# Three one-pass products on split operands in place of the four-pass float32 v projection, with x loaded by pairs

## Chip, cores and metric

One core of one Trainium2 chip. The metric is the time of one execution on the device, in microseconds (us), as the median of several runs; less is better. TensorE is called PE in the profile, VectorE DVE, ScalarE ACT, GpSimd POOL. In this kernel matmuls write tiles in PSUM, and all other tiles lie in SBUF; these are the two on-chip memories. The granted clock is the share of TensorE's full clock that the profile records as allowed.

## The reference

128 batches of a 128 x 512 matrix x go through two layers. All is float32.

```python
# layer 0: r = relu(b + the largest of the 512 columns of adj @ x), one value per row; x = layernorm(x + r)
# layer 1: multi-head attention of 8 heads under the mask adj, then a layer norm added to itself
qkv = x @ w_qkv                                  # 512 -> 3 x 512
attn = softmax(where(adj == 0, -inf, q @ k.T / 8))
o = (attn @ v).reshape(...) @ w_proj + b_proj
o = o + layernorm(o) * ln_gamma + ln_beta
x = layernorm(x + o)
```

The change is about v, the last third of `qkv`.

## The kernel before

The kernel is a software pipeline: in stage s it finishes batch s (transposed scores, attention, projection, two layer norms), computes the scores and the softmax of batch s+1, and the q, k, v of a group of batches 5 stages ahead. TensorE's order is written out by hand; the other engines' orders are made by a scheduler, and each engine runs its own list strictly in order.

```python
for s in range(-A_CONV, B):                 # TensorE's order
    ...
    if here:  eT = transpose_e(s)
    if nxt:   scores(s + 1)                 # psc, mask add, maximum, 8 exponentials
    if dense: qk(u // G, u % G)
    if here:  oT = attend(s, eT)            # pav, copied to oT by ScalarE
    if dense: qk(u // G, KC + u % G)
    if here:  project(s, oT)                # po, then VectorE's o and the layer norms
    if dense: vproj(u // G, u % G)
    if 0 <= t < B: transpose_x(t)
    if w < B: conv(w)

def vproj(g, i):                            # the part that the change rewrites
    xT = xTs[g]
    ...
    for kc in range(KC):                    # KC = 4 float32 matmuls of 512 columns
        nc.tensor.matmul(pv, xT[:, kc, i, :], wqkv_sb[:, kc, 2 * D :],
                         start=(kc == 0), stop=(kc == KC - 1))
    nc.scalar.copy(vs[g][:, i, :], pv)

def scores(b):
    ...
    nc.vector.tensor_tensor(e, psc..., mask_b, op=ALU.add)           # "mask add"
    nc.vector.tensor_reduce(nmax, e, AX.X, ALU.max, negate=True)     # "maximum"
    for j in range(H):                                               # 8 exponentials
        nc.scalar.activation(e[:, j, :], e[:, j, :], AF.Exp, bias=nmax[:, j : j + 1], ...)
    ...

def attend(b, eT):
    ...
    nc.scalar.copy(oT, pav)                 # the copy that project() needs
    return oT

def project(b, oT):
    ...                                     # po = oT @ wproj
    nc.vector.tensor_tensor(o, po, bproj_sb, op=ALU.add)
    nc.gpsimd.tensor_tensor(res, xs[g][:, i, :], o, op=ALU.add)
    stats(...); rstd = rstd_of(...)         # rstd: a small power on GpSimd
    nc.vector.scalar_tensor_tensor(o, o, mv..., gamma_sb, ...)       # "gamma pass"
    nc.vector.scalar_tensor_tensor(o, o, rstd, beta_sb, ...)         # "beta pass"
    nc.vector.tensor_tensor(y, res, o, op=ALU.add)                   # "y"
    stats(...); rstd2 = ...; nc.vector.tensor_scalar(y, ...)         # second layer norm
    nc.sync.dma_start(out[b], y)
```

## Time and profile before

| | before |
|---|---|
| time | 2415.31 us median of 4 runs (2410.86 to 2418.89) |
| TensorE busy | 98% of the span |
| one stage in the steady state | 18.42 us |
| mean granted TensorE clock | 0.995 |

The page's groups have the columns: line, engine, operation, output and inputs, shape and count; then busy us and mean ns of one; then the idle time of the engine just before such instructions, and what ended most of it. Two groups of the kernel before:

```profile
L208 ACT ACTIVATE e<-e,nmax 128x128 f32<-128x128 f32 x1024 | 395.9, 388 | 329.7 <-DVE nmax L205 327.2
L244 PE MATMUL po<-wproj_sb,oT 128*128 128x512 f32 x1024 | 463.1, 595 | 3.7 <-ACT oT L237 3.7
```

### The profile page before, as it was taken

The numbers are of one execution on the slowest core, as the hardware profiler recorded it, in microseconds if no ns is written. First come the engines' busy times: TensorE is split into PE (matmuls) and PEld (weight loads), VectorE is DVE, ScalarE is ACT, GpSimd is POOL, SyncE is SP. The second block draws the span as 40 slices with busy tenths as digits, with TensorE's granted clock in tenths as the row PEclk, the third lists the DMA queues.
The fourth block names the chain that finished last, engine by engine and source line by source line (L and its number), as shares of the span: only waits on it lengthen the run. The fifth ranks groups of instructions, "written<-read, shape, count | busy, mean of one in ns | idle before, by whom it ended". The sixth has DMA issues, their size and how long they took to land.

```text
span 2410.0 us, 27354 instructions
## 1 busy us (share of the span) xinstructions
PE 2368.1 (98%) x9985; PEld 1214.1 (50%) x9985; DVE 1550.2 (64%) x2755; ACT 806.2 (33%) x2689; POOL 333.5 (14%) x422
## 2 busy tenths in 40 slices
PE   7999999999999999999999999999999999999995
PEld 3455555555555555555555555555555555555543
DVE  3576666667666766666676667666666766666556
ACT  1333333333333333333333333333333333333332
POOL 0011111111111111111111111111111111111112
PEclk9999999999999999999999999999999999999998
DMA  5000001000000000000000000000000000000000
GB/s 206 5 31 35 14 31 36 31 31 24 25 31 31 31 36 14 31 35 31 31 21 28 31 31 31 36 14 31 35 31 31 21 29 14 14 14 18 14 18 22
DMA packets 38294, 73.91 MB, mean 31 GB/s; under 512 B 2832, under 2 KB 2960, under 8 KB 38160
## 3 DMA queue, kind: packets, MB, share of 16 engines
q1 hardware_dynamic: 35328, 67.12, 7.8%
q10 hardware_dynamic: 2832, 5.05, 0.6%
q8 instruction: 79, 1.29, 0.2%
q14 instruction: 55, 0.45, 0.1%
HBM read 38.60 MB, written 33.55 MB: 30 GB/s over the span
## 4 chain that ended last, share of the span: by engine, by line
PE 97%; DVE 1%; DMA 0%; ACT 0%; POOL 0%; issue 0%; POOLq 0%; SPq 0%; ACTq 0%; DVEq 0%
PE pq L168 38%; PE pv L183 18%; PE po L244 18%; PE psc L198 6%; PE pav L232 5%; PE ppt L221 5%; PE pa L132 4%; PE ptx L157 2%; DMA xt<-in_x_dram 0%; DVE st L121 0%; ACT e L208 0%; DVE e L214 0%; DVE o L248 0%; POOL res L250 0%; POOL rstd L116 0%
## 5 line engine op out<-in xcount | busy, mean ns | idle before, releaser
L168 PE MATMUL pq<-xT,wqkv_sb 128*128 128x512 f32 x2048 | 945.6, 605 | 0.0
L168 PEld LDWEIGHTS pq<-xT,wqkv_sb 128*128 128x128 f32 x2048 | 368.6, 189 | 408.0 <-issue 392.1
L208 ACT ACTIVATE e<-e,nmax 128x128 f32<-128x128 f32 x1024 | 395.9, 388 | 329.7 <-DVE nmax L205 327.2
L244 PE MATMUL po<-wproj_sb,oT 128*128 128x512 f32 x1024 | 463.1, 595 | 3.7 <-ACT oT L237 3.7
L183 PE MATMUL pv<-wqkv_sb,xT 128*128 128x512 f32 x1024 | 460.3, 592 | 0.0
L187 ACT COPY v<-pv 128x512 f32<-128x512 f32 x128 | 75.0, 586 | 941.7 <-PE pv L183 941.7
L250 POOL TENSOR_TENSOR res<-xt,o 128x512 f32<-128x512 f32 x128 | 162.0, 1266 | 1377.5 <-DVE o L248 984.6
L244 PEld LDWEIGHTS po<-wproj_sb,oT 128*128 128x128 f32 x1024 | 194.6, 191 | 249.6 <-issue 233.5
L183 PEld LDWEIGHTS pv<-wqkv_sb,xT 128*128 128x128 f32 x1024 | 194.6, 190 | 244.9 <-issue 244.9
L116 POOL TENSOR_TENSOR rstd<-ve,mhalf 128x1 f32<-128x1 f32 (+1 forms) x288 | 175.8, 610 | 694.9 <-DVE ve L114 694.5
L248 DVE TENSOR_TENSOR o<-po,bproj_sb 128x512 f32<-128x512 f32 x128 | 88.3, 690 | 269.2 <-PE po L244 269.2
L213 DVE RECIPROCAL rsum<-sums 128x8 f32<-128x8 f32 x128 | 25.7, 200 | 316.1 <-ACT e L208 316.1
L208 ACT ACTIVATION_READ_ACCUMULATOR e<-e,nmax 128x1 f32 x1024 | 191.2, 187 | 0.0
L223 ACT COPY eT<-ppt 128x1024 f32<-128x1024 f32 x128 | 129.6, 1012 | 149.0 <-PE ppt L221 149.0
L214 DVE TENSOR_TENSOR e<-e,rsum 128x1024 f32<-128x1024 f32 x128 | 158.0, 1234 | 4.3
L221 PEld LDWEIGHTS ppt<-ident,e 128*128 128x128 f32 x1024 | 119.4, 141 | 79.7 <-issue 65.0
L232 PEld LDWEIGHTS pav<-eT,v 128*64 128x64 f32 x2048 | 111.0, 138 | 95.5 <-issue 93.7
L205 DVE TENSOR_REDUCE nmax<-e 128x8 f32<-128x1024 f32 x128 | 156.2, 1220 | 3.3
L203 DVE TENSOR_TENSOR e<-psc,mask 128x1024 f32<-128x1024 f32 x128 | 155.0, 1211 | 1.7 <-PE psc L198 1.7
L198 PE MATMUL psc<-qkT 64*128 64x128 f32 x2048 | 150.6, 287 | 0.0
L221 PE MATMUL ppt<-ident,e 128*128 128x128 f32 x1024 | 133.0, 273 | 13.8 <-DVE mv L122 13.8
L175 DVE COPY qkT<-pq 128x512 f32<-128x512 f32 x128 | 88.2, 689 | 85.6 <-PE pq L168 85.3
(34 smaller groups left out, 1745.0 us busy)
## 6 DMA issues: line engine op xcount, KB each, us to landing
xt<-in_x_dram SPq DMA_DIRECT2D x32, 1024.0 KB, 5.4
out_dram<-y SPq DMA_DIRECT2D x128, 256.0 KB, 2.0
wqkv_sb<-in_L_gnn_w_qkv_dram ACTq DMA_DIRECT2D x3, 1024.0 KB, 16.3
wproj_sb<-in_L_gnn_w_proj_dram ACTq DMA_DIRECT2D x1, 1024.0 KB, 23.1
bproj_sb<-in_L_gnn_b_proj_dram ACTq DMA_DIRECT2D x1, 256.0 KB, 17.7
gamma_sb<-in_L_gnn_ln_gamma_dram ACTq DMA_DIRECT2D x1, 256.0 KB, 17.7
beta_sb<-in_L_gnn_ln_beta_dram ACTq DMA_DIRECT2D x1, 256.0 KB, 15.1
adj_sb<-in_adj_dram ACTq DMA_DIRECT2D x1, 64.0 KB, 2.4
```

Source lines behind the costliest of these rows:

```text
L116: nc.gpsimd.tensor_tensor(r, ve, mhalf[:, :n], op=ALU.pow)
L168: nc.tensor.matmul(pq, wqkv_sb[:, kc, c * P : (c + 1) * P], xT[:, kc], start=(kc == 0), stop=(kc == KC - 1),)
L183: nc.tensor.matmul(pv, xT[:, kc, i, :], wqkv_sb[:, kc, 2 * D :], start=(kc == 0), stop=(kc == KC - 1),)
L198: nc.tensor.matmul(psc[:, s, hp, :], qkT[hs, hp, i, :], qkT[hs, KC + hp, i, :], start=True, stop=True,)
L203: nc.vector.tensor_tensor(e, psc.rearrange("p s a m -> p (s a) m"), mask_b, op=ALU.add)
L205: nc.vector.tensor_reduce(nmax, e, AX.X, ALU.max, negate=True)
L208: nc.scalar.activation(e[:, j, :], e[:, j, :], AF.Exp, bias=nmax[:, j : j + 1], accum_out=sums[:, j : j + 1],)
L214: nc.vector.tensor_tensor(e, e, rsum[:, :, None].to_broadcast([P, H, P]), op=ALU.mult)
L221: nc.tensor.transpose(ppt[:, j, :], e[:, j, :], ident)
L232: nc.tensor.matmul(pav[s * HD : (s + 1) * HD, hp, :], vs[g][:, i, h * HD : (h + 1) * HD], eT[:, s * HP + hp, :], start=True, stop=True,)
L244: nc.tensor.matmul(po, oT[:, c, :], wproj_sb[:, c, :], start=(c == 0), stop=(c == KC - 1),)
L250: nc.gpsimd.tensor_tensor(res, xs[g][:, i, :], o, op=ALU.add)
```

## The change

The intent: a float32 matmul makes four passes. Split both operands exactly, x = h + l/4096 and w = wh + wl, each half of at most 12 bits, so that one pass of the faster float32 type (float32r) is meant to be exact. Three products, h·wh and l·wl added in one PSUM bank and d·wd in another, give v by Karatsuba's identity, three passes instead of four: (1 + 1/4096)(h·wh + l·wl) - (h - l)(wh - 4096 wl)/4096 = (h + l/4096)(wh + wl), with d = h - l and wd = wh - 4096 wl. Beside it, x is loaded and normalised by pairs of batches instead of by fours.

```diff
-        xt = xpool.tile([P, G, D], FP, tag="xt", name=f"xt_{g}")
-        nc.sync.dma_start(xt, x[g * G : (g + 1) * G].rearrange("b t d -> t b d"))
+        xt = xpool.tile([P, 2, D], FP, tag="xt", name=f"xt_{p}")
+        nc.sync.dma_start(xt, x[2 * p : 2 * p + 2].rearrange("b t d -> t b d"))
 ...
+    for c in range(KC):                               # weights, once
+        wv = work.tile([P, D], FP, tag="x4", name=f"wv_{c}")
+        nc.scalar.dma_start(wv, w_qkv[c * P : (c + 1) * P, 2 * D :])
+        wh = work.tile([P, D], FP, tag="xh", name=f"wh_{c}")
+        nc.vector.tensor_scalar(wh.bitcast(I32), wv.bitcast(I32), HIGH, None, op0=ALU.bitwise_and)
+        nc.scalar.copy(wv_h[:, c], wh)
+        nc.vector.tensor_tensor(wv_l[:, c], wv, wh, op=ALU.subtract)
+        nc.vector.scalar_tensor_tensor(wv_d[:, c], wv_l[:, c].bitcast(FP), -HALF, wh, ...)
 ...
+    def split_x(b):                                   # every batch
+        nc.scalar.activation(x4, xTs[g][:, :, i, :], AF.Copy, scale=HALF)
+        nc.vector.tensor_scalar(xh.bitcast(I32), x4.bitcast(I32), HIGH, None, op0=ALU.bitwise_and)
+        nc.scalar.activation(h, xh, AF.Copy, scale=1.0 / HALF)
+        nc.gpsimd.tensor_tensor(l, x4, xh, op=ALU.subtract)
+        nc.gpsimd.tensor_tensor(d, h.bitcast(FP), l.bitcast(FP), op=ALU.subtract)
 ...
     def vproj(g, i):
+            nc.tensor.matmul(pv, h[:, kc], wv_h[:, kc], start=(kc == 0), stop=False)
+            nc.tensor.matmul(pv, l[:, kc], wv_l[:, kc], start=False, stop=(kc == KC - 1))
 ...
-                pv, xT[:, kc, i, :], wqkv_sb[:, kc, 2 * D :],
+                pd, d[:, kc], wv_d[:, kc], start=(kc == 0), stop=(kc == KC - 1),
 ...
-        nc.scalar.copy(vs[g][:, i, :], pv)
+        nc.scalar.activation(va, pv, AF.Copy, scale=1.0 + 1.0 / HALF)
+        nc.vector.scalar_tensor_tensor(vs[g][:, i, :], pd, -1.0 / HALF, va, ...)   # "v"
 ...                                  # conv(): statistics after every 2nd batch, not every 4th
-        if i < G - 1:
+        if i == 0:
             return
 ...                                  # work tiles: 1 buffer instead of 2, o and oT 2, y 2 instead of 4
+            if 0 <= s + A_SPLIT < B:
+                split_x(s + A_SPLIT)
```

More of the change, by code (lines that the diff above doesn't have):

```diff
@@ L12 @@
 AX = mybir.AxisListType
+FR = mybir.dt.float32r
+I32 = mybir.dt.int32
 H = 8
@@ L16 @@
 MASKED = -1e30
+HIGH = -4096
+HALF = 4096.0
 @with_exitstack
@@ L58, in tile_adj_resnorm_d2 @@
     const = ctx.enter_context(tc.tile_pool(name="const", bufs=1))
-    xpool = ctx.enter_context(tc.tile_pool(name="xpool", bufs=7))
+    xpool = ctx.enter_context(tc.tile_pool(name="xpool", bufs=9))
     group = ctx.enter_context(tc.tile_pool(name="group", bufs=2))
-    work = ctx.enter_context(tc.tile_pool(name="work", bufs=2))
+    split = ctx.enter_context(tc.tile_pool(name="split", bufs=3))
+    work = ctx.enter_context(tc.tile_pool(name="work", bufs=1))
     small = ctx.enter_context(tc.tile_pool(name="small", bufs=4))
@@ L64, in tile_adj_resnorm_d2, with load_x @@
     ps_2 = ctx.enter_context(tc.tile_pool(name="ps_2", bufs=2, space=bass.MemoryType.PSUM))
-    xs, rs, qkTs, vs, xTs, es, mv0s = {}, {}, {}, {}, {}, {}, {}
-    def load_x(g):
-        xt = xpool.tile([P, G, D], FP, tag="xt", name=f"xt_{g}")
-        nc.sync.dma_start(xt, x[g * G : (g + 1) * G].rearrange("b t d -> t b d"))
-        xs[g] = xt
+    xs, rs, qkTs, vs, xTs, es, mv0s, splits = {}, {}, {}, {}, {}, {}, {}, {}
+    def load_x(p):
+        xt = xpool.tile([P, 2, D], FP, tag="xt", name=f"xt_{p}")
+        nc.sync.dma_start(xt, x[2 * p : 2 * p + 2].rearrange("b t d -> t b d"))
+        xs[p] = xt
     adj_sb = const.tile([P, P], FP, name="adj_sb")
@@ L77, in tile_adj_resnorm_d2 @@
     nc.scalar.dma_start(b0_sb, b0.rearrange("(p o) -> p o", o=1))
-    load_x(0)
-    wqkv_sb = const.tile([P, KC, 3 * D], FP, name="wqkv_sb")
-    for j in range(3):
+    for p in range(3):
+        load_x(p)
+    wqk_sb = const.tile([P, KC, 2 * D], FP, name="wqk_sb")
+    for j in range(2):
         nc.scalar.dma_start(
-            wqkv_sb[:, :, j * D : (j + 1) * D],
+            wqk_sb[:, :, j * D : (j + 1) * D],
             w_qkv[:, j * D : (j + 1) * D].rearrange("(c p) f -> p c f", p=P),
+        )
+    wv_h = const.tile([P, KC, D], FR, name="wv_h")
+    wv_l = const.tile([P, KC, D], FR, name="wv_l")
+    wv_d = const.tile([P, KC, D], FR, name="wv_d")
+    for c in range(KC):
[5 more added lines that the diff above has]
+        nc.vector.tensor_tensor(wv_l[:, c], wv, wh, op=ALU.subtract)
+        nc.vector.scalar_tensor_tensor(
+            wv_d[:, c], wv_l[:, c].bitcast(FP), -HALF, wh, op0=ALU.mult, op1=ALU.add,
         )
@@ L125, in conv @@
     def conv(b):
-        g, i = divmod(b, G)
-        xt = xs[g]
+        p, i = divmod(b, 2)
+        xt = xs[p]
         if i == 0:
-            rs[g] = small.tile([P, G], FP, tag="r", name=f"r_{g}")
+            rs[p] = small.tile([P, 2], FP, tag="r", name=f"r_{p}")
         pa = ps_1.tile([P, D], FP, tag="ps1", name=f"pa_{b}")
         nc.tensor.matmul(pa, adjT, xt[:, i, :], start=True, stop=True)
-        nc.vector.tensor_reduce(rs[g][:, i : i + 1], pa, AX.X, ALU.max)
-        if i < G - 1:
+        nc.vector.tensor_reduce(rs[p][:, i : i + 1], pa, AX.X, ALU.max)
+        if i == 0:
             return
-        r = rs.pop(g)
+        r = rs.pop(p)
         nc.vector.tensor_scalar(r, r, b0_sb, 0.0, op0=ALU.add, op1=ALU.max)
-        mv = small.tile([P, G, 2], FP, tag="mv0", name=f"mv0_{g}")
-        for j in range(G):
+        mv = small.tile([P, 2, 2], FP, tag="mv0", name=f"mv0_{p}")
+        for j in range(2):
             nc.vector.tensor_scalar(xt[:, j, :], xt[:, j, :], r[:, j : j + 1], None, op0=ALU.add)
-            stats(mv[:, j, :], xt[:, j, :], f"0_{g}_{j}")
-        mv0s[g] = mv, rstd_of(mv, G, f"0_{g}")
+            stats(mv[:, j, :], xt[:, j, :], f"0_{p}_{j}")
+        mv0s[p] = mv, rstd_of(mv, 2, f"0_{p}")
     def transpose_x(b):
         g, i = divmod(b, G)
-        xt = xs[g]
-        mv, rstd = mv0s[g]
+        j = b % 2
+        xt = xs[b // 2][:, j, :]
+        mv, rstd = mv0s[b // 2]
         if i == 0:
@@ L151, in transpose_x @@
         nc.vector.tensor_scalar(
-            xt[:, i, :], xt[:, i, :], mv[:, i, 0:1], rstd[:, i : i + 1],
-            op0=ALU.subtract, op1=ALU.mult,
+            xt, xt, mv[:, j, 0:1], rstd[:, j : j + 1], op0=ALU.subtract, op1=ALU.mult,
         )
@@ L156, in transpose_x @@
         for c in range(KC):
-            nc.tensor.transpose(pt[:, c, :], xt[:, i, c * P : (c + 1) * P], ident)
+            nc.tensor.transpose(pt[:, c, :], xt[:, c * P : (c + 1) * P], ident)
         nc.scalar.copy(xTs[g][:, :, i, :], pt)
+    def split_x(b):
+        g, i = divmod(b, G)
+        x4 = work.tile([P, KC, P], FP, tag="x4", name=f"x4_{b}")
+        nc.scalar.activation(x4, xTs[g][:, :, i, :], AF.Copy, scale=HALF)
+        xh = work.tile([P, KC, P], FP, tag="xh", name=f"xh_{b}")
+        nc.vector.tensor_scalar(xh.bitcast(I32), x4.bitcast(I32), HIGH, None, op0=ALU.bitwise_and)
+        h = split.tile([P, KC, P], FR, tag="h", name=f"h_{b}")
+        nc.scalar.activation(h, xh, AF.Copy, scale=1.0 / HALF)
+        l = split.tile([P, KC, P], FR, tag="l", name=f"l_{b}")
+        nc.gpsimd.tensor_tensor(l, x4, xh, op=ALU.subtract)
+        d = split.tile([P, KC, P], FR, tag="d", name=f"d_{b}")
+        nc.gpsimd.tensor_tensor(d, h.bitcast(FP), l.bitcast(FP), op=ALU.subtract)
+        splits[b] = h, l, d
     def qk(g, c):
@@ L168, in qk @@
             nc.tensor.matmul(
-                pq, wqkv_sb[:, kc, c * P : (c + 1) * P], xT[:, kc],
+                pq, wqk_sb[:, kc, c * P : (c + 1) * P], xT[:, kc],
                 start=(kc == 0), stop=(kc == KC - 1),
@@ L177, in vproj @@
     def vproj(g, i):
-        xT = xTs[g]
+        h, l, d = splits.pop(g * G + i)
         if i == 0:
@@ L182, in vproj @@
         for kc in range(KC):
+            nc.tensor.matmul(pv, h[:, kc], wv_h[:, kc], start=(kc == 0), stop=False)
+            nc.tensor.matmul(pv, l[:, kc], wv_l[:, kc], start=False, stop=(kc == KC - 1))
+        pd = ps_1.tile([P, D], FP, tag="ps1", name=f"pd_{g}_{i}")
+        for kc in range(KC):
             nc.tensor.matmul(
-                pv, xT[:, kc, i, :], wqkv_sb[:, kc, 2 * D :],
-                start=(kc == 0), stop=(kc == KC - 1),
-            )
-        nc.scalar.copy(vs[g][:, i, :], pv)
+                pd, d[:, kc], wv_d[:, kc], start=(kc == 0), stop=(kc == KC - 1),
+            )
+        va = work.tile([P, D], FP, tag="va", name=f"va_{g}_{i}")
+        nc.scalar.activation(va, pv, AF.Copy, scale=1.0 + 1.0 / HALF)
+        nc.vector.scalar_tensor_tensor(
+            vs[g][:, i, :], pd, -1.0 / HALF, va, op0=ALU.mult, op1=ALU.add,
+        )
     def scores(b):
@@ L235, in attend @@
                 )
-        oT = work.tile([P, HP, P], FP, tag="oT", name=f"oT_{b}")
+        oT = work.tile([P, HP, P], FP, bufs=2, tag="oT", name=f"oT_{b}")
         nc.scalar.copy(oT, pav)
@@ L246, in project @@
             )
-        o = work.tile([P, D], FP, tag="o", name=f"o_{b}")
+        o = work.tile([P, D], FP, bufs=2, tag="o", name=f"o_{b}")
         nc.vector.tensor_tensor(o, po, bproj_sb, op=ALU.add)
         res = work.tile([P, D], FP, tag="res", name=f"res_{b}")
-        nc.gpsimd.tensor_tensor(res, xs[g][:, i, :], o, op=ALU.add)
+        nc.gpsimd.tensor_tensor(res, xs[b // 2][:, b % 2, :], o, op=ALU.add)
         mv = small.tile([P, 1, 2], FP, tag="mv1", name=f"mv1_{b}")
@@ L258, in project @@
         nc.vector.scalar_tensor_tensor(o, o, rstd, beta_sb, op0=ALU.mult, op1=ALU.add)
-        y = work.tile([P, D], FP, tag="y", name=f"y_{b}", bufs=4)
+        y = work.tile([P, D], FP, tag="y", name=f"y_{b}", bufs=2)
         nc.vector.tensor_tensor(y, res, o, op=ALU.add)
@@ L268, in project @@
         nc.sync.dma_start(out[b], y)
-    A_DENSE, A_TRANS, A_CONV = 5, 9, 14
+    A_DENSE, A_SPLIT, A_TRANS, A_CONV, A_LOAD = 5, 6, 9, 11, 14
     with tc.manual_schedule(engines={mybir.EngineType.PE}):
@@ L275, in tile_adj_resnorm_d2 @@
             here, nxt = 0 <= s, 0 <= s + 1 < B
-            u, t, w = s + A_DENSE, s + A_TRANS, s + A_CONV
+            u, t, w, f = s + A_DENSE, s + A_TRANS, s + A_CONV, s + A_LOAD
             dense = 0 <= u < B
-            if w % G == 0 and w // G + 1 < NG:
-                load_x(w // G + 1)
+            if f % 2 == 0 and 6 <= f < B:
+                load_x(f // 2)
             if here:
```

## The prediction

> **What bounds the kernel now.** I read the page first, then the chain of waits, then the timeline of one stage on TensorE, VectorE (DVE) and ScalarE (ACT), and last the end of the run, where engines overlap in an unusual way.
>
> ```profile
> PE 2368.1 (98%) x9985; PEld 1214.1 (50%) x9985; DVE 1550.2 (64%) x2755; ACT 806.2 (33%) x2689; POOL 333.5 (14%) x422
> PE 97%; DVE 1%; DMA 0%; ACT 0%; POOL 0%; issue 0%; POOLq 0%; SPq 0%; ACTq 0%; DVEq 0%
> L183 PE MATMUL pv<-wqkv_sb,xT 128*128 128x512 f32 x1024 | 460.3, 592 | 0.0
> ```
>
> TensorE is 98% busy and is 97% of the chain that ended last, so TensorE work bounds the kernel. The v projection, which the change rewrites, is 460 us of it: 128 batches x 4 chunks = 512 matmuls, shown as 1024 records.
>
> The steady state repeats per batch. A stage in the timeline of TensorE, then of ACT, then of DVE:
>
> ```profile
> 1035.38 3.60 PE L244 MATMUL po<-wproj_sb,oT 128*128 128x512 f32 x8
> 1038.81 3.60 PE L183 MATMUL pv<-wqkv_sb,xT 128*128 128x512 f32 x8
> 1042.25 0.60 PE L157 MATMUL ptx<-ident,xt 128*128 128x128 f32 x4
> ...
> 1053.80 3.60 PE L244 MATMUL po<-wproj_sb,oT 128*128 128x512 f32 x8
> ```
>
> ```profile
> 1048.38 0.40 ACT L208 ACTIVATE e<-e,nmax 128x128 f32<-128x128 f32 x1 [2.69 <-DVE nmax L205]
> ...
> 1051.47 0.57 ACT L173 ACTIVATE qkT<-pq 128x512 f32<-128x512 f32 x1
> 1051.95 0.57 ACT L237 COPY oT<-pav 128x512 f32<-128x512 f32 x1
> ```
>
> ```profile
> 1039.01 0.69 DVE L248 TENSOR_TENSOR o<-po,bproj_sb 128x512 f32<-128x512 f32 x1 [2.74 <-PE po L244]
> ...
> 1042.01 0.75 DVE L258 SCALAR_TENSOR_TENSOR o<-o,rstd,beta_sb 128x512 f32<-128x512 f32 x1
> 1042.79 0.69 DVE L260 TENSOR_TENSOR y<-res,o 128x512 f32<-128x512 f32 x1
> ...
> 1044.54 0.68 DVE L133 TENSOR_REDUCE r<-pa 128x1 f32<-128x512 f32 x1
> 1045.35 0.55 DVE L265 TENSOR_SCALAR y<-y,mv,rstd 128x512 f32<-128x512 f32 x1
> 1045.81 1.22 DVE L203 TENSOR_TENSOR e<-psc,mask 128x1024 f32<-128x1024 f32 x1
> 1047.06 1.22 DVE L205 TENSOR_REDUCE nmax<-e 128x8 f32<-128x1024 f32 x1
> ```
>
> A stage is 1053.80 - 1035.38 = 18.42 us. The reader should see a second, hidden loop: po(s) ends, DVE does o(s) and the layer norm, only then the mask add and maximum of the next scores; ACT then does 8 exponentials and only after them oT(s+1), which po(s+1) needs. From o's start (1039.01) to oT's end (1052.52) is 13.51 us; TensorE arrives at po at 14.79. So this loop has only 1.28 us of slack, though DVE is 64% busy and ACT 33%.
>
> The end of the run shows one thing more (DVE, then GpSimd):
>
> ```profile
> 2375.68 1.21 DVE L214 TENSOR_TENSOR e<-e,rsum 128x1024 f32<-128x1024 f32 x1
> 2387.59 1.84 DVE L214 TENSOR_TENSOR e<-e,rsum 128x1024 f32<-128x1024 f32 x1
> ```
>
> ```profile
> 2374.45 1.26 POOL L250 TENSOR_TENSOR res<-xt,o 128x512 f32<-128x512 f32 x1 [2.00 <-DVE o L248]
> 2387.09 1.26 POOL L250 TENSOR_TENSOR res<-xt,o 128x512 f32<-128x512 f32 x1 [3.48 <-DVE rsum L213]
> ```
>
> The same multiply takes 1.21 us when GpSimd's add ends as it starts, and 1.84 us when the add covers its first 0.76 us. It stood still until the add was nearly over.
>
> **What the Trainium skill says.** "FP8 and Floating Point Precision", TensorE Precision Notes: true FP32 takes four passes. "TensorE: Matmul & The Clock Gate", Part 1: back-to-back 512-column matmuls start 215.7 ns apart. The trace agrees with both: pv's 8 records take 1042.25 - 1038.81 = 3.44 us, 0.43 each, two passes of 0.215 per record, four per matmul. "SBUF — State Buffer", SBUF: two separate sides: a GpSimd instruction and a DVE instruction with two SBUF inputs (or in a two-port mode) exclude each other for the whole instruction. The 1.84 us above agrees. The TensorE page, Part 1, also halves the clock after about 3.4 us of idling; the trace agrees roughly (scores at the end of the run take 1.98 to 2.08 us after 3.5 us of idling, 1.16 otherwise).
>
> **The change, part by part.**
>
> TensorE: four passes become three. 12 one-pass matmuls at an estimated 0.215 us (the trace has no one-pass 512-column matmul) = 2.58 us against 3.44: 0.86 us less per stage, 110 us in all. TensorE alone would need 17.56 us a stage and reach po 13.93 us after o's start. By TensorE alone the kernel would take about 2310 us.
>
> ACT gains two 128x512 passes per batch at 0.58 us (148 us in all); one beside its idle time after xT, the other between oT and the v copy. Not on the loop.
>
> GpSimd gains two 128x512 subtractions at 1.27 us (the res row), 324 us in all. The built program puts both between the two small rstd of the two layer norms.
>
> DVE gains the bit mask (0.47 us, as the 128x512 tensor_scalar of L140) and the v combination from PSUM (about 0.75), 156 us in all, for 71% of the new span. But the built order puts both **ahead of the mask add**, inside the loop: o, statistics, two layer-norm passes, v, y, conv maximum, statistics, bit mask, y's normalisation, mask add, maximum. On ACT oT now stands after the exponentials in **every** stage; before, the stages with conv statistics (one in four) had oT ahead of them.
>
> The loop, from o's start, with the start-to-start distances of the trace (neighbours that don't depend on each other overlap by 0.07): gamma pass 2.14, beta pass 3.00, v 3.68, y 4.36, conv maximum 4.98, statistics 5.59, bit mask 6.20, aggregate 6.65, epsilon 6.86, normalise y 7.74 (0.88 for GpSimd's rstd, with nothing left to do meanwhile), mask add 8.21, against 6.80 before: **+1.41 us**.
>
> Now the lock. GpSimd: res ends at 2.08, rstd at 2.60; the first subtraction waits for the gamma pass and runs 2.74 to 4.01; the beta pass (two SBUF inputs) gets through at 3.87 instead of 3.00; the second subtraction then runs 4.47 to 5.74; v reads PSUM and passes, y has two SBUF inputs and starts at 5.60 instead of 4.36: **+1.24 us**. Mask add at 9.45; then as before 1.25 to the maximum, 1.31 to the first exponential, 3.09 for eight, 0.48 for qkT, 0.57 for oT, about 0.08 to po: po starts at 16.2, against 13.93 when TensorE is free. With 3.63 us from po's start to o's (1039.01 - 1035.38) the stage is 19.85 us.
>
> Every second stage also has the pair's conv statistics. Before nmax they put r, two adds (0.4 each) and two statistics (0.6 each) in the way, partly filling the rstd wait: +1.66 us; qkT stands before the exponentials there (-0.48). Stage: 21.0 us.
>
> Mean 20.4 us, +2.0 over 18.42. About 123 stages have full density: +245 us. The start: the v weights come in four loads through a single-buffered tile, each waiting for DVE, and ACT's order puts the last x transposes after them; I estimate the first q/k matmul at about 40 us instead of 26.6, less 4 us for the five cheaper prologue stages: +10. The clock: gaps of 3.4 us in every second stage may cost some TensorE clock, +10 by choice. 2418.6 + 265 = about **2680 us**.
>
> The new weight split (8 passes of DVE and 4 of ACT) is within the start. Loading x by pairs moves 0.5 MB at a time, three stages ahead of its use (over 50 us against 5.4 us to land): hidden either way.
>
> **The rivals.**
>
> *TensorE stays the bound*: 2310 to 2420 us. For it: 98% busy now and 0.86 us less per stage. Against it: a slack of 1.28 us that has to take in 1.41 us of added DVE work alone, while TensorE arrives 0.86 earlier.
>
> *The loop binds without the lock*: stages of 18.6 and 19.8, mean 19.2, about 2525 us. For it: in the steady state before, the small rstd on GpSimd ran beside a two-input pass without harm. Against it: the 1.84 us row.
>
> *More blocking*: if the second subtraction goes ahead of the beta pass, or v is held as well, another 0.65 us a stage, about 2760 us; with the clock dropping in most gaps, 2800.
>
> *The one-pass matmul is not one pass*: at 0.43 us each, v would take 5.2 us, and TensorE would reach po at 15.6, still inside the loop's 16.2; the time would hardly change.
>
> *Single buffers* (e, res, bit-mask input, va): the orders show each one's last reader done before its next writer; no wait expected.
>
> **Range and chances.** 2680, and 2540 to 2790 holds the loop without lock but with some extra, up to more blocking. Faster by over 2%: 0.05, which needs the whole loop reading to be wrong. Within 2%: 0.07. Slower by over 2%: 0.88.
>
> **What would show it.** TensorE busy at about 2240 us but only some 84% of the span, with idle time before po released by ACT's oT, near 2.2 and 3.4 us in alternating stages. pv and pd records near 0.215 us apart. DVE's beta pass and y longer than 0.75 and 0.69 us when GpSimd's l and d run. The chain no longer 97% TensorE but shared with DVE and ACT exponentials. The prediction is wrong if po's idle time is small, if beta and y keep their durations, or if the first full stage comes after 100 us.

## More of the kernel before

In 128 projections TensorE waited 3.7 us in all for oT. The exponentials do wait for VectorE's maximum, but ScalarE has the time.

## The result, and the profile after

The changed kernel is correct and takes **2705.55 us** (median of 4 runs, 2704.4 to 2708.2), against 2415.31 us: a ratio of 1.1204, 95% interval 1.1179 to 1.123. A ratio here and below is the mean time of one kernel's fast runs over the mean of the other's fast runs of the same rounds, so it is not quite the ratio of the medians. The prediction of 2680 us (2540 to 2790) holds.

From the page of the changed kernel, the busy times, the chain that ended last by engine, and four groups:

```profile
PE 2388.6 (88%) x10497; PEld 1328.4 (49%) x10497; DVE 1801.2 (67%) x3087; ACT 969.7 (36%) x2949; POOL 740.7 (27%) x710
PE 33%; DVE 29%; ACT 18%; issue 10%; POOL 10%; DMA 1%; DVEq 0%; POOLq 0%; ACTq 0%
L294 PE MATMUL po<-wproj_sb,oT 128*128 128x512 f32 x1024 | 537.3, 673 | 258.8 <-ACT oT L287 258.7
L200 POOL TENSOR_TENSOR d<-h,l 128x512 fp32r<-128x512 f32 x128 | 202.7, 1583 | 10.1
L308 DVE SCALAR_TENSOR_TENSOR o<-o,rstd,beta_sb 128x512 f32<-128x512 f32 x128 | 194.6, 1521 | 14.7 <-POOL rstd L144 1.8
```

The chain is no longer TensorE's: it is shared by all four engines, which is what a loop through all four looks like. TensorE waits 258.8 us ahead of po where it waited 3.7, all for ScalarE's oT. The beta pass takes 1521 ns on average; before it took 0.75 us. And po itself takes 673 ns per record where it took 595. That is 537.3 - 463.1 = 74 us of TensorE time that no instruction explains.

The timeline of TensorE (start us, duration us, engine, line, operation, [idle before <- releaser]), three projections in a row:

```profile
999.66 3.70 PE L294 MATMUL po<-wproj_sb,oT 128*128 128x512 f32 x8 [2.73 <-ACT oT L287]
...
1004.12 0.40 PE L226 MATMUL pv<-wv_h,h 128*128 128x512 f32 x1
1004.36 0.40 PE L227 MATMUL pv<-wv_l,l 128*128 128x512 f32 x1
...
1019.24 3.70 PE L294 MATMUL po<-wproj_sb,oT 128*128 128x512 f32 x8 [1.54 <-ACT oT L287]
...
```

The stage from 999.66 to 1019.24 is 19.58 us; the next, with the statistics of a pair of batches, ends with the po at 1039.99 and is 20.75 us. TensorE stands still for 1.54 us ahead of one po and for 2.73 or 2.72 ahead of the other. The two one-pass matmuls shown start 0.24 us apart; 0.233 is the mean of such distances.

The loop itself in the stage of 19.58 us, on VectorE, GpSimd and ScalarE:

```profile
1003.40 0.69 DVE L298 TENSOR_TENSOR o<-po,bproj_sb 128x512 f32<-128x512 f32 x1 [2.16 <-PE po L294]
...
1006.35 1.57 DVE L308 SCALAR_TENSOR_TENSOR o<-o,rstd,beta_sb 128x512 f32<-128x512 f32 x1
1007.85 0.68 DVE L235 SCALAR_TENSOR_TENSOR v<-pd,va 128x512 f32<-128x512 f32 x1
1008.45 1.16 DVE L310 TENSOR_TENSOR y<-res,o 128x512 f32<-128x512 f32 x1
...
1012.54 1.22 DVE L253 TENSOR_TENSOR e<-psc,mask 128x1024 f32<-128x1024 f32 x1
```

```profile
1005.94 1.44 POOL L198 TENSOR_TENSOR l<-x,xh 128x512 fp32r<-128x512 f32 x1
1007.46 1.61 POOL L200 TENSOR_TENSOR d<-h,l 128x512 fp32r<-128x512 f32 x1
```

```profile
1015.05 0.40 ACT L258 ACTIVATE e<-e,nmax 128x128 f32<-128x128 f32 x1 [5.68 <-DVE nmax L255]
...
1018.62 0.57 ACT L287 COPY oT<-pav 128x512 f32<-128x512 f32 x1
```

The mask add comes 1012.54 - 1003.40 = 9.14 us after o; before it came 6.80 us after. The beta pass (two inputs in SBUF) ends at 1007.92, 0.54 us after GpSimd's l at 1007.38. y (two inputs in SBUF) ends at 1009.61, 0.54 us after GpSimd's d at 1009.07. Between them v, which reads PSUM, passes in its usual 0.68 us. ScalarE has stood idle for 5.68 us when the maximum is ready, does eight exponentials and a copy of q, and only then the copy of oT, although the attention output pav was finished at 1014.06 (1012.97 + 1.09 on TensorE). The copy is a wait in a queue, not for data: it could have run 4.5 us earlier.

**Where the 293.5 us of the span went** (2703.5 less 2410.0). The first po starts at 111.84 us instead of 96.22: 15.6 us. In the 113 stages after it the mean stage is 20.69 us instead of 18.41: 258 us. The last stages, which have less and less to do, lose the other 20 us. Of these 20.69 us the loop alone would give (19.58 + 20.75) / 2 = 20.17. The other 0.52 us a stage is po running slowly: 34 of the 128 projections took 5.1 to 6.7 us instead of 3.70, 64 us more in all. Of the 59 that came after a gap of 2.65 to 2.9 us, 32 were slow; of the other 69, 2 were.

Why only some of these gaps did it can be read from the record of the granted clock, which runs in windows of 3.41 us. Between 112 and 2600 us the clock fell to half 33 times, for one or two windows. In the window before the fall TensorE had stood idle for 2.02 to 2.74 us, and once for 1.93; in the 656 full-speed windows that no fall followed, never for more than 1.99. A gap of 2.7 us thus slows the next projection when about 2 us of it lie in one window, and does not when a window's edge divides it more evenly. The mean granted clock fell from 0.995 to 0.963.

### The profile page after: what moved, and what is told of

Read it like the earlier page. It is cut to its first block, busy times and chain, and to the rows that moved or that the text cites. A ratio compares the mean times of both kernels' runs of the same rounds, so it can differ in the third digit from the quotient of the medians.

```text
span 2703.5 us, 29366 instructions
## 1 busy us (share of the span) xinstructions
PE 2388.6 (88%) x10497; PEld 1328.4 (49%) x10497; DVE 1801.2 (67%) x3087; ACT 969.7 (36%) x2949; POOL 740.7 (27%) x710
## 3 DMA queue, kind: packets, MB, share of 16 engines
q10 hardware_dynamic: 2880, 5.05, 0.5%
## 4 chain that ended last, share of the span: by engine, by line
PE 33%; DVE 29%; ACT 18%; issue 10%; POOL 10%; DMA 1%; DVEq 0%; POOLq 0%; ACTq 0%
PE po L294 20%; ACT e L258 14%; DVE nmax L255 5%; DVE e L253 5%; DVE st L149 4%; POOL d L200 3%; POOL res L300 3%; POOL rstd L144 3%; DVE y L310 2%; DVE y L315 2%; PE pv L227 2%; PE pd L230 2%; PE pv L226 2%; ACT oT L287 2%; PE pa L160 2%
## 5 line engine op out<-in xcount | busy, mean ns | idle before, releaser
L211 PE MATMUL pq<-xT,wqk_sb 128*128 128x512 f32 x2048 | 945.7, 605 | 1.6 <-ACT xT L186 1.6
L294 PE MATMUL po<-wproj_sb,oT 128*128 128x512 f32 x1024 | 537.3, 673 | 258.8 <-ACT oT L287 258.7
L211 PEld LDWEIGHTS pq<-xT,wqk_sb 128*128 128x128 f32 x2048 | 368.6, 189 | 409.8 <-issue 374.6
L196 ACT ACTIVATE h<-xh 128x512 fp32r<-128x512 f32 x128 | 80.9, 632 | 735.3 <-PE pv L226 731.8
L226 PE MATMUL pv<-wv_h,h 128*128 128x512 f32 x512 | 253.4, 495 | 0.0
L200 POOL TENSOR_TENSOR d<-h,l 128x512 fp32r<-128x512 f32 x128 | 202.7, 1583 | 10.1
L308 DVE SCALAR_TENSOR_TENSOR o<-o,rstd,beta_sb 128x512 f32<-128x512 f32 x128 | 194.6, 1521 | 14.7 <-POOL rstd L144 1.8
L227 PE MATMUL pv<-wv_l,l 128*128 128x512 f32 x512 | 202.0, 395 | 0.0
L198 POOL TENSOR_TENSOR l<-x,xh 128x512 fp32r<-128x512 f32 x128 | 183.3, 1432 | 29.3 <-PE pv L227 27.1
L216 ACT ACTIVATE qkT<-pq 128x512 f32<-128x512 f32 x128 | 75.0, 586 | 233.4 <-PE pq L211 233.4
```

The costliest lines, as they stand in the source:

```text
L198: nc.gpsimd.tensor_tensor(l, x4, xh, op=ALU.subtract)
L200: nc.gpsimd.tensor_tensor(d, h.bitcast(FP), l.bitcast(FP), op=ALU.subtract)
L211: nc.tensor.matmul(pq, wqk_sb[:, kc, c * P : (c + 1) * P], xT[:, kc], start=(kc == 0), stop=(kc == KC - 1),)
L226: nc.tensor.matmul(pv, h[:, kc], wv_h[:, kc], start=(kc == 0), stop=False)
L227: nc.tensor.matmul(pv, l[:, kc], wv_l[:, kc], start=False, stop=(kc == KC - 1))
L294: nc.tensor.matmul(po, oT[:, c, :], wproj_sb[:, c, :], start=(c == 0), stop=(c == KC - 1),)
```

## The experiments

The theory at this point: a loop (po, o, layer norms, mask add, maximum, exponentials, oT copy, po) bounds the kernel. It was lengthened by VectorE's new work, by GpSimd's subtractions holding VectorE's two-input instructions, and by the statistics coming in every second stage. The gaps it makes then slow the clock. The rivals: the load or the blocking on VectorE and GpSimd binds by itself (any order of ScalarE gives about the same time); or the buffers, of which there are fewer, do.

### e1: the oT copy ahead of the exponentials

```diff
-        nc.scalar.copy(oT, pav)
+        cp = nc.scalar.copy(oT, pav)
 ...
+    def softmax(b, e, nmax, oT_copy):       # split off from scores(), called after attend(); oT_copy is cp
 ...
+            ex = nc.scalar.activation(
 ...
+                tc.add_manual_dep(ex.ins, oT_copy.ins.name, ISSUE_ORDER, reason="oT first")
```

> The changed kernel with one thing moved: ScalarE issues the copy oT(s) ahead of the exponentials of batch s+1, in every stage; DVE's order stays, except that the second qkT copy goes ahead of the reciprocal. My theory (the loop po, layer norm, v and mask, mask add, exponentials, oT, po sets the stage): the loop is cut, TensorE sets the stage again, 14.99 us of unchanged work plus 2.79 for v as measured in the changed kernel = 17.8 us; total about 2350 us, 13% faster than the changed kernel and 2 to 3% faster than before; idle before po near zero; DVE's beta pass and y still 1.5 and 1.1 us long. Rival 1 (the added work on DVE and GpSimd, with their mutual blocking, is itself the bound): little changes, 2650 to 2720. Rival 2 (the single buffers, or eight PSUM tiles per stage in four banks): unchanged, 2705.

Measured: 2352.79 us, ratio to before 0.9751 (0.9734 to 0.9768).

```profile
PE 2294.7 (98%) x10497; PEld 1315.1 (56%) x10497; DVE 1800.0 (76%) x3087; ACT 991.4 (42%) x2949; POOL 739.8 (31%) x710
L300 PE MATMUL po<-wproj_sb,oT 128*128 128x512 f32 x1024 | 462.6, 594 | 3.4 <-ACT oT L293 3.4
L314 DVE SCALAR_TENSOR_TENSOR o<-o,rstd,beta_sb 128x512 f32<-128x512 f32 x128 | 194.5, 1519 | 14.7 <-POOL rstd L145 1.8
```

```profile
1014.17 0.59 ACT L293 COPY oT<-pav 128x512 f32<-128x512 f32 x1 [0.44 <-PE pav L288]
1016.77 0.40 ACT L262 ACTIVATE e<-e,nmax 128x128 f32<-128x128 f32 x1 [2.01 <-DVE nmax L256]
```

The manual dependency sets the order on ScalarE only, without a semaphore. This one edge is worth some 350 us; beside it, VectorE's second copy of qkT went ahead of the reciprocal, as the expectation says. The copy now starts 0.05 us after pav ends (1013.03 + 1.09 on TensorE). All the work is still there, and the beta pass is blocked as long as before (1519 ns), but TensorE is 98% busy, waits 3.4 us in all ahead of po, and po is back at 594 ns. The stage is 17.77 us (po at 999.82 and 1017.59), which is 18.42 less 0.64 us. So the blocking by itself binds nothing, nor do the buffers: both rivals fall. The blocking cost time only because oT was queued behind what it delayed. This is also the first version that is faster than the kernel before.

### e5: the same edge in the kernel before

```diff
-        nc.scalar.copy(oT, pav)
+        cp = nc.scalar.copy(oT, pav)
 ...
+                tc.add_manual_dep(ex.ins, oT_copy.ins.name, ISSUE_ORDER, reason="oT first")
```

> The kernel before with the same order as in the first experiment: oT ahead of the exponentials in every stage. My theory: TensorE already bounds it and its loop has 1.28 us of slack, so the order is worth nothing here: 2412 within 1%. It follows that the 13% that the order gained in the changed kernel are not a gain of the order as such. Rival (the order is a gain of its own, the change has nothing to do with it): 2360 or less.

Measured: 2416.43 us, ratio 1.0012 (0.9991 to 1.0034). As expected: where the loop has slack, the order is worth nothing. The gain of e1 is not a general gain of the edge.

### e2: no subtractions on GpSimd

The two subtractions are left out and constants of the same shape go to TensorE. v is wrong on purpose; it still passed the tolerance, so the correctness check says nothing about l and d here.

```diff
-        nc.gpsimd.tensor_tensor(l, x4, xh, op=ALU.subtract)
-        nc.gpsimd.tensor_tensor(d, h.bitcast(FP), l.bitcast(FP), op=ALU.subtract)
+        l = wv_l[:, 0].rearrange("p (c q) -> p c q", c=KC)
+        d = wv_d[:, 0].rearrange("p (c q) -> p c q", c=KC)
```

> The changed kernel without GpSimd's two subtractions (constants of the same type stand in for l and d, so the result is wrong on purpose); orders on DVE and ScalarE stay. My theory: DVE's beta pass back to 0.75 us (-0.82) and y back to 0.69 (-0.47, of which part is overlap), mask add 1.2 us earlier, stage 1.2 us shorter, -145 us, and about 50 us of lost TensorE clock comes back as the gaps before po get shorter than 2 us: about 2510 us. Rival 1 (no mutual blocking matters, only the instruction counts): unchanged within 1%. Rival 2 (single buffers, PSUM): unchanged.

Measured: 2490.97 us, ratio 1.0326 (1.0311 to 1.0342). The timeline of VectorE:

```profile
1003.63 0.69 DVE L296 TENSOR_TENSOR o<-po,bproj_sb 128x512 f32<-128x512 f32 x1 [2.16 <-PE po L292]
...
1006.65 0.75 DVE L306 SCALAR_TENSOR_TENSOR o<-o,rstd,beta_sb 128x512 f32<-128x512 f32 x1
...
1007.92 0.68 DVE L308 TENSOR_TENSOR y<-res,o 128x512 f32<-128x512 f32 x1
...
1011.54 1.22 DVE L251 TENSOR_TENSOR e<-psc,mask 128x1024 f32<-128x1024 f32 x1
```

With nothing on GpSimd beside them, the beta pass and y are back at 0.75 and 0.68 us, and the mask add comes 7.91 us after o instead of 9.14: 1.23 us, the 1.24 us that the prediction gave the blocking. The gaps ahead of po fall to 1.50 and 0.32 us, and gaps that short left the clock alone: of the 128 projections only the last was slow. The ratios differ by 1.1204 - 1.0326 = 0.088, so blocking and the clock loss that it brings about are some 210 us of the 290. The rest is the loop without the blocking: VectorE's added work and the statistics by pairs, with oT behind the exponentials, and the later start.

### e3 and e9: v queued behind the maximum, with and without the subtractions

v (0.68 us on VectorE) lies inside the loop. Is it worth 0.68 us a stage?

```diff
+            v = nc.vector.scalar_tensor_tensor(
+                vs[g][:, i, :], pd, -1.0 / HALF, va, op0=ALU.mult, op1=ALU.add,
+            )
 ...
+                tc.add_manual_dep(v.ins, after.ins.name, ISSUE_ORDER, reason="v late")   # after: the maximum of the scores
```

> The changed kernel with DVE's v combination queued behind the maximum of the scores, so that it leaves the loop; all work stays. My theory: the v combination (0.68 us) sat in the shadow of GpSimd's second subtraction, which holds y anyway, so nothing is gained: 2705 within 1%. The rival that the added DVE instructions simply add up (0.68 us a stage) expects -84 us or more, 2620.

e3 measured: 2733.61 us, ratio 1.1334 (1.1316 to 1.1352). The additive rival (2620) fails. The theory's total is missed narrowly, on the slow side, and in a telling way.

```profile
1017.54 0.69 DVE L306 TENSOR_TENSOR o<-po,bproj_sb 128x512 f32<-128x512 f32 x1 [5.16 <-PE po L302]
...
1022.10 1.65 DVE L318 TENSOR_TENSOR y<-res,o 128x512 f32<-128x512 f32 x1
...
1026.65 1.22 DVE L260 TENSOR_TENSOR e<-psc,mask 128x1024 f32<-128x1024 f32 x1
```

Without v ahead of it, y starts 0.5 us earlier in the loop (4.56 us after o, not 5.05), and is blocked for 0.5 us longer (1.65 us, not 1.16). The mask add comes 9.11 us after o; with v it was 9.14. v had been free, done while y would have had to wait for GpSimd anyway. The extra 28 us came from elsewhere: moving v made the scheduler put the statistics of a pair wholly ahead of the mask add in every second stage, and the gap there grew from 2.72 to 3.07 us. The slow projections lose some 13 us more than without the edit.

Then v should count as soon as nothing blocks y. That is e9.

> GpSimd's two subtractions replaced by constants, as in e2, and VectorE's combine of v queued behind the conv maximum, as in e3. Theory (v was hidden only because VectorE stood[...] behind GpSimd's subtraction; with no subtraction there is no shadow, so v's own 0.68 us counts): the mask addition of an even stage comes about 0.6 us earlier than in e2 (7.91 us after o, to about 7.3), and the total falls from e2's 2491 to about 2455 us (2440 to 2470; not all of 132 times 0.65, as the order of the odd stages was worse by some 0.3 us when v moved in e3). Rival (v costs nothing on the path in any order, the loss is the subtractions alone): 2485 to 2500 us.

(The edit is that of e3, behind the maximum of the scores.) e9 measured: 2454.56 us, ratio 1.0153 (1.0138 to 1.0168), against 1.0326 of e2. As expected. The mask add of an ordinary stage comes 7.40 us after o instead of 7.91. The same edit costs 28 us with the subtractions and gains about 0.017 x 2415 = 42 us without them.

### e4: the pairs alone

The kernel after with the four-pass v of the kernel before; the loading, normalising and buffers of the change stay.

```diff
-            nc.tensor.matmul(pv, h[:, kc], wv_h[:, kc], start=(kc == 0), stop=False)
-            nc.tensor.matmul(pv, l[:, kc], wv_l[:, kc], start=False, stop=(kc == KC - 1))
 ...                                            # pd, va, v and split_x() go too
+            nc.tensor.matmul(pv, xT[:, kc, i, :], wqkv_sb[:, kc, 2 * D :], ...)
+        nc.scalar.copy(vs[g][:, i, :], pv)
```

> Only the other half of the change: x by pairs, the new buffer counts and leads, v by the old four-pass product. My theory: stages without conv statistics bound by TensorE at 18.42 us; in every second stage the pair's statistics put the mask add at 9.15 us after o's start and oT's end at 15.8, against TensorE's arrival at 14.8, so +1.1 us there; mean 18.97, +68 us: about 2485 us. Rival (buffers or pair loading cost a wait in every stage): over 2550. Rival (pairs are free): 2410 to 2425.

Measured: 2487.65 us, ratio 1.0306 (1.0289 to 1.0324). In every second stage:

```profile
1030.38 3.70 PE L258 MATMUL po<-wproj_sb,oT 128*128 128x512 f32 x8 [0.84 <-ACT oT L251]
...
1048.90 3.60 PE L258 MATMUL po<-wproj_sb,oT 128*128 128x512 f32 x8
```

Before, the statistics of four batches stood in one stage of four, and there the scheduler had put oT ahead of the exponentials. By pairs they stand in one of two, with oT behind the exponentials; the mask add then comes 9.06 us after o, and 6.73 in the stages between. So working by pairs, with the buffers that go with it, costs 76 us by itself (2487.65 less the 2411.12 of before in the same rounds). It had nothing to give in return: DMA was 0% of the chain before.

### e6 and e7: how much slack the kernel before has

One and three useless additions of 128 x 512 on VectorE between the beta pass and the mask add, in the kernel before.

```diff
+        for _ in range(1):          # 3 in e7
+            nc.vector.tensor_tensor(junk, o, gamma_sb, op=ALU.add)
```

> The kernel before with one useless 128x512 addition of DVE (0.69 us) a stage between the beta pass and y. My theory: it fits into the slack of 1.28 us in all stages but those after conv statistics, where o already starts 0.28 us late: 2412 to 2425. A rival that says DVE's time counts in full: +0.62 x 123 = 76 us, 2490.

e6 measured: 2447.28 us, ratio 1.0145 (1.0129 to 1.016): missed. The mask add came 1.05 us later (7.85 us after o), not 0.62, since the maximum of the convolution had run during the wait for GpSimd's power and now no longer did. An ordinary stage still did not wait: its 18.41 us show that 1.05 us is within the slack. The 25.6 us that TensorE waited for oT lie in 37 of the 128 stages, chiefly those after a stage with statistics, where the slack is smaller.

> The kernel before with three such additions (about 1.8 us a stage on DVE's way from o to the mask add). My theory: past the slack. In two of four stages 1.8 - 1.28 = 0.5 us of waiting, in the stage after conv statistics (twice delayed) about 2.6, with oT ahead of the exponentials in the fourth none: 3.6 us per four stages, 108 us in all, about 2520 (2480 to 2550), with DVE still only about 73% busy. A rival that sees DVE's share of busy time alone (64% plus 9%) expects no change.

e7 measured: 2567.58 us, ratio 1.0649 (1.0633 to 1.0665): the direction is right and the size too small. The mask add came 1.98 us later, the ordinary stage waits 0.60 us (19.27 us), the one after the statistics 2.61. Delay less wait is 1.98 - 0.60 = 1.38 us: the slack of the ordinary stage, which the prediction had read as 1.28.

### e8, e10 and e11: the start

e1 starts late. Its first matmul of q and k is at 44.7 us against 26.6 before. e8 is e1 with the weights of v loaded by one transfer and split whole, instead of in four pieces through one buffer.

```diff
-    for c in range(KC):
-        wv = work.tile([P, D], FP, tag="x4", name=f"wv_{c}")
-        nc.scalar.dma_start(wv, w_qkv[c * P : (c + 1) * P, 2 * D :])
+    wv = group.tile([P, KC, D], FP, tag="v", name="wv")
+    nc.scalar.dma_start(wv, w_qkv[:, 2 * D :].rearrange("(c p) f -> p c f", p=P))
```

> The changed kernel with oT ahead of the exponentials, and the v weights loaded by one transfer into the two buffers of v, so that their split is one chain instead of four loads through one buffer. My theory: the first q/k matmul comes at about 30 us instead of 44.7, all else as in the first experiment: about 2340 us (2335 to 2345), 3% faster than before. If the start isn't bound by those loads: 2353.

e8 measured: 2357.81 us, ratio 0.9774 (0.9759 to 0.9789): wrong. The bit mask of the weights now stands early in VectorE's list, and with it everything behind:

```profile
23.27 1.23 DVE L107 TENSOR_SCALAR wh<-wv 128x2048 int32<-128x2048 int32 x1 [13.31 <-DMA wv<-in_L_gnn_w_qkv_dram]
```

"PSUM — Partial Sum Buffer" of the Trainium skill, Engine vs sequencer instructions, calls the queues of ScalarE, VectorE and GpSimdE strict first-in-first-out; here VectorE stands for 13.31 us with ready work right behind the bit mask (the relu of r, whose inputs were done at 9.96 us), which agrees. e10 keeps the one transfer and queues the splitting of the weights behind the normalisation of the fourth batch.

```diff
+        tc.add_manual_dep(first.ins, after_x[0].ins.name, ISSUE_ORDER, reason="x first")   # bit mask, VectorE
+        tc.add_manual_dep(cast.ins, after_x[1].ins.name, ISSUE_ORDER, reason="x first")    # cast, ScalarE
```

> The change with the oT copy issued ahead of the exponentials (e1), the weights of v by one transfer, and the splitting of those weights queued behind the normalisation of the third batch of x, so that no engine stands waiting for the weights at the head. Theory (e1 lost about 15 us at the head, since the first x operations waited in their engines' queues behind the weights of v): the first q/k matmul starts near 30 us instead of 45, and the total is about 2338 us (2332 to 2345), some 3 per cent under the kernel before. Rival (x's own loads by pairs set the head, not the weights): as e1, 2350 to 2358 us.

e10 measured: 2349.28 us, ratio 0.9716 (0.97 to 0.9733): better than e1, but the first q/k matmul is at 40.07 us, not near 30, and the total is just outside the range. What stood in the way:

```profile
23.25 0.34 ACTq L127 DMA_DIRECT2D beta_sb<-in_L_gnn_ln_beta_dram  x1
23.61 1.28 ACT L195 ACT_TABLE_LOAD   x1 [23.61 <-DMA wv<-in_L_gnn_w_qkv_dram]
```

ScalarE issues the transfers of the weights itself and got its last one out only at 23.25 us, so it copied the first xT only after that. Issuing is the small part of this: its nine issues take 4.8 us together. The last one waited; the profile puts the wait down to wv, which was issued at 4.60 and landed 18.6 us later. And the splits of the first two batches stood ahead of the normalisation of the second pair. e11 takes both away:

```diff
-    nc.scalar.dma_start(wproj_sb, ...)         # and the three row vectors
+    nc.sync.dma_start(wproj_sb, ...)
+        if b == 0:
+            tc.add_manual_dep(up.ins, after_x[1].ins.name, ISSUE_ORDER, reason="x first")
```

> As e10, with two more edits at the head: ScalarE no longer issues the transfers of the projection weights and of the three row vectors (SyncE does, behind the first three loads of x), and the splitting of the first batch is queued behind the normalisation of the fourth. e10 left the first q/k matmul at 40.07 us: ScalarE issued its last row transfer at 23.25 us and copied its first xT only at 24.91, and the splits of two batches stood ahead of the normalisation of the second pair on VectorE and GpSimd. Theory (these two are what was left of the late start): first q/k matmul between 26 and 31 us and 2334 to 2342 us in all. Rival (the later loads of x or the weights of q and k set the head): first q/k matmul after 36 us, 2345 to 2350 us.

e11 measured: **2340.54 us**, ratio 0.9684 (0.9668 to 0.9701), as expected; the rival (x or the q and k weights set the start) falls.

```profile
29.05 7.14 PE L223 MATMUL pq<-xT,wqk_sb 128*128 128x512 f32 x16
```

How much each of the two edits gave was not separated. e11 is the best version found: the change with an order that suits it, 3.2% below the kernel before and 13.6% below the change as it stood (0.9684 / 1.1204 = 0.864).

## Why the prediction was right

- **Which loop, and that it binds.** Right. The chain is shared by TensorE, VectorE, ScalarE and GpSimd as it said, and e1, which shortens nothing and only moves oT out of the loop, turns 2705 us into 2353.
- **The added VectorE work and the blocking.** Right in mechanism and in size. The mask add was put at 9.45 us after o and is at 9.14; the blocking was put at 1.24 us and e2 measures 1.23. The order of the working was too simple in one place. It counted v as a cost of its own ahead of the blocking of y, and e3 shows that, with y blocked anyway, v cost 0.03 us. The sum was right, because it had taken y's delay from the end of GpSimd's d.
- **The stages.** 19.85 and 21.0 us were predicted and 19.58 and 20.75 are measured, without slow projections. That is a mean of 20.17, not 20.4: the loop's term is about 1.75 x 123 = 215 us, not 245 (123 stages, as the prediction counted). Most of the difference is small: the bit mask takes 0.32 us from start to start instead of 0.45, the wait for GpSimd's power 0.82 instead of 0.88.
- **The clock.** The mechanism was named, the size is the step that failed. "+10 by choice" measured about 64. It was a choice and not worked out from anything. The gaps are in every second stage, as predicted, and shorter than predicted (2.7 us, not 3.4), and still more than half of them slow the next projection: what the runs show to matter is about 2 us of idling within one window of 3.41 us. One reading behind this term is wrong too: at the end of the run the 1.98 us belong to pav (1.09 otherwise), not to the scores, and the scores at 2366.86 take their usual 1.16 us after 3.35 us of idling. 30 us too much in the loop, 54 too little here and 6 too little at the start nearly cancel. That the total is only 25 us low is in part luck.
- **The start.** 10 us were predicted and 15.6 are measured on the first po: the weights go through one buffer, each transfer waiting for VectorE, and the last of their four casts ran at 36.53 us in the changed kernel. e11 shows that this is mostly order, not work. The prediction had named a first full stage after 100 us as a sign of being wrong; the first stage that finishes a batch begins at 101.59 us (85.97 before), so this sign did appear, by 6 us of start and not by the loop.
- **TensorE's saving.** Mis-sized, without consequence: the trace of the changed kernel has 2.56 us from the start of the second one-pass matmul (1003.43) to that of the next work (1005.99), eleven of them, so 0.233 each and 2.79 us for twelve, not 2.58; v saves 0.64 us a stage, not 0.86. e1 confirms it, where TensorE is the bound (17.77 us against 18.42). The estimate of 2310 us with TensorE alone as the bound was too low by this; the best run here has 2340.54.
- **TensorE's busy share.** 2240 us at 84% was predicted (its own terms, 2368 - 110, give 2258), and 2388.6 us at 88% is measured. e1, which has the same matmuls without the gaps, is busy for 2294.7 us. The other 94 us come with the gaps, and 75 of them are po's (537.3 against 462.6 us).
- **Sums that do not come out.** If the matmuls were not one pass, v's 5.16 us would bring TensorE to po at 13.93 + 2.58 = 16.5 us, past the loop's 16.2, and not at 15.6; the runs show one pass, so nothing rests on it. VectorE's 71% is a share of the old span; of the predicted one it is (1550 + 156) / 2680 = 64%. 67% is measured, which includes the time in which its instructions stand blocked.
- **The rivals.** "TensorE stays the bound" and "the loop binds without the lock" (2525 us) fall; the second is nearly e2's 2491 us, where the lock is taken away. "More blocking" did not come: v takes its 0.68 us. "Single buffers" falls with e1, which keeps them all.

## What to carry to other kernels

When TensorE is 98% busy, measure the slack of the next loop before taking work off TensorE: here it was about 1.3 us of 18.4, and helper work of 0.4 to 1.6 us each on VectorE and GpSimd used it up. Then look for an instruction that stands in a queue behind others that it does not need; moving that one copy was worth more than all of the change's arithmetic. And an instruction that reads PSUM may be free where its neighbour with two SBUF inputs stands blocked by GpSimd, so test a move in the presence of the lock, not by its own duration.

## What the Trainium skill lacked or had wrong

- "TensorE: Matmul & The Clock Gate", Part 1, gives 215.7 ns from start to start for 512 columns. The float32 passes agree (0.215 us each), but float32r matmuls, each with its own weight load, start 0.233 us apart here (12 in 2.79 us).
- The same part has the clock fall after an idle window of about 3.4 us. Here the windows have that length (3.41 us), but one need not be idle throughout: 32 of the 33 falls counted above followed a window with 2.02 to 2.74 us of idle time, and none of the windows without a fall had more than 1.99. Gaps of 2.65 to 2.9 us were thus enough in 32 of 59 cases (po 5.1 to 6.7 us instead of 3.70).
- "FP8 and Floating Point Precision", TensorE Precision Notes, has the four passes of float32 and a reduced-precision read, but no time for the latter and no word on exact splitting: three products cost 2.79 us against 3.44 for the four-pass form.
- "SBUF — State Buffer", SBUF: two separate sides, has whichever of the two starts first hold the other up, and the runs agree in both directions. What the page does not say is how a profile shows it: as a longer held instruction, not as idle time before it. In e11 a subtraction on GpSimd that started 0.03 us after a two-input pass of VectorE took 3.38 us instead of 1.27. In turn it and the subtraction after it held two of VectorE's tensor-scalar passes (2.91 us for two, 0.88 for two such passes at 19.90):

```profile
30.37 2.29 DVE L118 SCALAR_TENSOR_TENSOR wv_d<-wv_l,wh 128x2048 fp32r<-128x2048 f32 x1
...
30.40 3.38 POOL L210 TENSOR_TENSOR l<-x,xh 128x512 fp32r<-128x512 f32 x1 [7.23 <-DVE xh L206]
32.57 2.91 DVE L177 TENSOR_SCALAR xt<-xt,r 128x512 f32<-128x512 f32 x2
```

- "Trainium Kernel Development and Optimization", Key Constraints, says that issuing transfers from several engines "only saves the sequencer's issue time". Here it saved more than that. In e10 ScalarE's nine issues take 4.8 us together, but its last came out at 23.25 us, because an issue in its queue waited for a transfer to land, and its compute stood behind it. With that transfer and three others on SyncE, and the split of the first batch later, the first q/k matmul came 11.0 us earlier (e11).
